# Load casts queued behind their neighbours, second-layer weights over slots 59 to 73, both ends in written order: one change to a two-layer cross-attention kernel

## The chip, the cores and the metric

The kernel runs on one core of one Trainium2 chip. The metric is the device time of one execution in microseconds (us). Five engines work side by side, each through its own instruction queue in order: PE (TensorE, matmuls; its weight loads are listed apart as PEld), DVE (VectorE), ACT (ScalarE), POOL (GpSimd) and SP (SyncE, which here only issues DMAs). ACT issues a few DMAs too. An instruction waits on semaphores for what it reads, and everything behind it on its engine waits with it.

## What is computed

The input is 16 batches of 256 rows and 320 channels, `x`, and a context of 256 rows and 512 channels for each batch. Two cross-attention layers follow each other, 20 heads of 16 channels each. In layer 1 the first 77 context rows are text and the other 179 image tokens; in layer 2 all but the last 4 are text.

```python
# layer 1 (L0)                                   # layer 2 (L1)
text_out = softmax(q_h k_h^T * s) v_h            text_out = softmax(q k_t^T * s) v_t
text_probs = softmax(q k_text^T * s)             qsem = l2norm(probs_t @ text_ehs)     # per head
sem = (text_probs @ text) @ ip^T * s             sem  = qsem @ l2norm(ip_ehs)^T
fused = q_h ip_k_h^T * s + 0.5 * sem             fused = q k_ip^T * s + 0.5 * sem
ip_out = softmax(fused) * mask @ ip_v_h          ip_out = softmax(fused) * mask @ v_ip
out = (text_out + ip_out) @ Wout + bout + x      out = (text_out + ip_out) @ W_out + b_out + x1
```

All is float32. The kernel keeps that precision by splitting operands into a rounded part and a rest (`hi` and `lo`, type fp32r) and multiplying hi by hi, hi by lo and lo by hi.

## The kernel before

**Slots.** A layer has 80 groups: 16 batches of 5 groups of 4 heads. The main loop (the last lines of the function) runs 162 slots, k = 0 to 161. Slot k of layer 1 is `slot0`, of layer 2 `slot1`; NS = 80 is the first slot of layer 2. In a slot, fixed steps stand at fixed places: `score0` or `both1` makes scores of group k+2 (PE L623 or L749) that DVE reduces to row maxima (L624, L625, L750); `maxima0` or `maxima1` turns the maxima with a small matmul (L631), ACT copies them to `mt` (L633), and ACT issues DMAs (L635) that put them into extra rows of `qs`; `turned0` makes the scores again, transposed (L647, tile T), ACT takes the exponential into P (L650), POOL multiplies P by `rs` (L651); `attend0` multiplies by the values (L678), and `settle0` scales the result on DVE. `stacks(k + LEAD)`, LEAD = 4, has SP issue the loads of `qs` and `ks` for a group four slots ahead.

**Tasks.** All else is a generator with a list of due times in slots: `task(key, times, make, *needs)`. `fill(now)` runs, in order of due time, every step that is due; `get` runs a task to its end. `("k0", c)` makes keys of a pair of batches, `q0` queries, `s0` the semantic scores (`rs`), `v0` values, `c0` and `c1` the output projection of a batch (PE L496, residual added in L723), `o1`, `k1`, `t1` the layer-2 inputs, and `i1` layer 2's image softmax (`image_softmax`, L852 to L883), whose result `rs` `close1` multiplies on PE at L892. `w1`, `w6`, `w2`, `w4` load and split weights.

**Loads and casts.** `dma` (L82) puts a load on SP's queue. `in_turn` loads parts of 128x512 into a ring of two raw buffers, then `halves` splits each: an ACT cast (L131), and a DVE or POOL subtraction (L132).

**What sets the order.** PE's queue is in the order written, since the main loop runs under a schedule that pins PE alone. For ACT, DVE, POOL and SP the scheduler chooses the order by times that it reckons while the program is built. The first stretch, `begin()`, pins PE and SP.

**Ends.** `begin()` makes keys, queries, semantic scores and values of the first batches, loads the first four stacks and makes the first maxima, before slot 0. At the other end, slots 160 and 161 finish the last two groups, and `fill(999)` the last image softmax and output projections.

**DVE, POOL and buffers touched.** `bmask` has a buffer of its own, loaded at the start; `settle1` takes a fresh half of `nt` for each group; batch 0's `x` is loaded twice, as `x0` for the queries and in `close0` as the residual.

Of the kernel before, what the change touches and what calls it, by code (L numbers as in the profile page):

```python
# [48 lines left out]
def xattn2(  # L49
# [80 lines left out]
    def halves(hi, lo, src, eng=nc.vector):  # L130
        nc.scalar.copy(hi, src)  # L131
        eng.tensor_sub(lo, src, f(hi))  # L132

    def in_turn(parts, wait, tag="raw", eng=nc.vector):

        ahead = []
        for src, hi, lo in list(parts) + [(None, None, None)]:
            if src is not None:
                raw = buf(tag, [128, 512], bufs=2)
                shape = src.shape  # L140
                raw = raw[:, : shape[1]] if len(shape) == 2 else raw.rearrange("p (k n) -> p k n", k=shape[1])
                dma(raw, src)
                ahead.append((hi, lo, raw))
            if len(ahead) > 1 or (src is None and ahead):
                halves(*ahead.pop(0), eng)
            if wait:
                yield
# [40 lines left out]
    def context(b, n, wait=0):  # L188

        tiles, parts = [], []  # L190
        for k in range(0, 4, 3 - n):
            src = cT_d[:, b * S : (b + n) * S].rearrange("(k p) t -> p k t", p=128)[:, k : k + 3 - n]
            ct = buf("cta" if n == 1 or k < 2 else "ctb", [128, 2, 512], FR, bufs=SIZES["CTA" if n == 1 or k < 2 else "CTB"], name="ct")
            split = lambda t: t.rearrange("p (k t) -> p k t", t=n * S)
            parts.append((src, split(ct[:, 0]), split(ct[:, 1])))
            tiles.append(ct)
        yield from in_turn(parts, wait, "rawc", nc.gpsimd if wait else nc.vector)
        if n == 2:
            return lambda s, k: tiles[k][:, s].rearrange("p (b t) -> p b t", b=2)
        return lambda s, k: tiles[k // 2][:, s, (k % 2) * S : (k % 2 + 1) * S]  # L200
# [65 lines left out]
    bmask = const_tile([128, CP], "bmask")  # L266
# [10 lines left out]
    def keys0(c):  # L277
        if c not in ct0:
            ct0[c] = yield from context(2 * c, 2, 0.25)
        ct = ct0[c]  # L280
        for m in range(3):
            ms = slice(m * 128, (m + 1) * 128)
            kst = buf("kst", [128, 2, 2, S], FR, bufs=SIZES["KST"])
            for w, lo, hi, a, z in ((wk0, 0, 96, 0, T0), (wki0, T0 - 1, S, T0, S)):
                kp = bank()[:, : 2 * (hi - lo)].rearrange("p (b t) -> p b t", b=2)
                prod(kp, lambda s, k: w(s, k, ms), lambda s, k: ct(s, k)[:, :, lo:hi], 4)
                halves(kst[:, 0, :, a:z], kst[:, 1, :, a:z], kp[:, :, a - lo : z - lo])
                if a:
                    keys_out(kd[0][c], m, kst)
                yield  # L290
# [50 lines left out]
    def weights1():  # L341
# [25 lines left out]
        halves(cip[:, 0], cip[:, 1], raw)  # L367
# [38 lines left out]
    def weights3():  # L406
        gm = buf("vr", [128, 3 * (H * V0W + 16)], FR, bufs=3, name="gm")
        gm = gm[:, : 7 * 128].rearrange("p (g n) -> p g n", n=128)
        nc.gpsimd.memset(f(gm), 0.0)
        gmt.append(gm)  # L410
        yield
        if len(gmt) == 2:
            one, two = [buf("rs", [128, 2 * S], bufs=2, name="one") for i in range(2)]
            w1["vb"], w1["mhalf"] = one[:, :CP], one[:, CP : CP + NG * 8]
            w1["pT"], w1["pip"] = two[:, :S], two[:, S:].rearrange("p (f c) -> p f c", c=32)
            dma(bmask, bmask_d)
            nc.vector.memset(w1["mhalf"], -0.5)
            nc.gpsimd.memset(w1["pip"], 0.0)
# [61 lines left out]
    def split(src, neg, eng, tag):  # L480

        hl = buf(tag, [128, 5, S], FR)
        nc.scalar.copy(hl[:, 0:3], src)
        eng.tensor_sub(hl[:, 3:5], src[:, 0:2], f(hl[:, 0:2]))
        nc.vector.scalar_tensor_tensor(  # L485
            hl[:, 2], f(hl[:, 2]), neg, src[:, 2], op0=ALU.mult, op1=ALU.add
        )
        return hl
# [125 lines left out]
    maxes = {}  # L614

    def score0(k, t):
        Q, K = QK[k]
        if t == 0:
            maxes[k] = buf("mn", [128, 2, 4, 2], FR, bufs=2)
        mn = maxes[k]  # L620
        sp = scores()
        for h in range(4):
            mm(sp[:, h], Q[: XROW + T0, h, t * 128 : (t + 1) * 128], K[: XROW + T0, h], start=True, stop=True)  # L623
        nc.vector.tensor_reduce(mn[:, t, :, 0], sp[:, :, :T0], axis=AX.X, op=ALU.max)  # L624
        nc.vector.tensor_reduce(mn[:, t, :, 1], sp[:, :, T0:], axis=AX.X, op=ALU.max)  # L625

    def maxima0(k):
# [6 lines left out]
        for h in range(4):  # L634
            nc.scalar.dma_start(f(Q[XROW + T0 : KS0, h]), f(mt[2 * h : 2 * h + 2]))  # L635

    def turned0(k, t):
# [10 lines left out]
        for p in range(2):  # L648
            pt = P[k, p][:, t]
            nc.scalar.activation(pt, st[p], AF.Exp, scale=SCALE)  # L650
            nc.gpsimd.tensor_mul(pt, pt, rs[:, t : t + 1].to_broadcast([128, 2, S]))  # L651
# [8 lines left out]
    def slot0(k):  # L660
# [4 lines left out]
        yield 0.2  # L665
        if k > 0:
            yield lambda: attend0(k - 1)
        yield lambda: ahead(k + 2, 1)
        yield lambda: turned0(k, 1)
        yield lambda: stacks(k + LEAD)  # L670
# [59 lines left out]
    def both1(k, t):  # L730
# [14 lines left out]
        if a:  # L745
# [4 lines left out]
            nc.vector.tensor_reduce(maxes[k + 2][:, t], sp[:, :, :T1], axis=AX.X, op=ALU.max)  # L750
        if c:
            for u in range(2):
                if t == 0:
                    P[k, u] = buf("P", [128, 2, 2, S], bufs=SIZES["NP"])
                nc.scalar.activation(P[k, u][:, t], st[u], AF.Exp, scale=SCALE)  # L755
# [13 lines left out]
    def rounded1(k, u):  # L769
        R[k, u] = buf("ctb", [128, 2, 2, S], FR, bufs=SIZES["CTB"], name="ph")  # L770
        W[k, u] = buf("wB", [128, 2, 2, S], bufs=SIZES["WB"], name="wt")
        for t in range(2):
            nc.scalar.activation(R[k, u][:, t], P[k, u][:, t], AF.Copy, scale=0.5)  # L773
            nc.gpsimd.tensor_sub(W[k, u][:, t], P[k, u][:, t], f(R[k, u][:, t]))  # L774
# [54 lines left out]
    def settle1(b, g, pv):  # L829
# [4 lines left out]
        na = buf("nt", [128, 2, 8, 32], bufs=2, name="na")[:, 0]  # L834
# [11 lines left out]
    def image_softmax(b):  # L846
        nt, si = norms[b], get("o1", b)[1]
        pool = nc.gpsimd
        small = lambda n, t: buf(t, [128, NG, 8] + ([n] if n > 1 else []))
# [7 lines left out]
        pool.tensor_tensor(r, u, w1["mhalf"].rearrange("p (f s) -> p f s", f=NG), op=ALU.pow)  # L857
        b4 = lambda t: t.unsqueeze(3).to_broadcast([128, NG, 8, NIP])
        a = small(NIP, "a")
        pool.tensor_mul(a, nt[:, :, :, 1:5], b4(r))  # L860
        by_group = lambda t: t[:, :, : NG * NIP].rearrange("p f (g n) -> p g f n", n=NIP)
# [13 lines left out]
        pool.tensor_mul(z4, z4, mk.unsqueeze(1).to_broadcast([128, NG, 8]))  # L875
        pi = w1["pip"]
        pool.tensor_mul(by_group(pi), a, b4(z4))
        vb = w1["vb"]
# [4 lines left out]
        nc.vector.tensor_mul(vb, vb, bmask)  # L883
# [15 lines left out]
    def close0(b):  # L899
        x1 = yield from finish(0, b, results["gathered", 0, b], load(xT_d[b], "xc"))  # L900
        dma(x1d[b].rearrange("(k p) t -> p k t", p=128), x1)

    def open1(b):
# [3 lines left out]
        yield  # L907
        qh, qd = yield from queries(1, xs)
# [57 lines left out]
    first_kt = []  # L966
# [7 lines left out]
    FIRST = {"k0": [-1, -1, -1, -1, -1, 0.6, 1, 1.2, 1.6, 2, 2.4], "s0": [-1, 0.2, 0.2, 0.6, 0.6, 1, 1.2]}  # L974
    for c in range(B // 2):
        n, k = 10 * c, [("k0", c)] if c else []
        task(("k0", c), FIRST["k0"] if c == 1 else shifted(n, -13, -12.6, -12.3, -12, -11.6, -10.8, -10.4, -9.8, -9.4, -8.8, -8.4), (lambda c=c: keys0(c)) if c else first_keys,
             *((("v0", 2 * c - 1), ("m0t", 2 * c - 1), *([("w4", 0)] if c > 1 else [])) if c else ()))
# [6 lines left out]
        for b, t in ((2 * c, (-7.4, -6.4, -6, -5.4, -5, -4.4, -3.4)), (2 * c + 1, (-2.4, -1.4, -1, -0.8, -0.4, 0, 1.2))):  # L985
            task(("s0", b), FIRST["s0"] if b == 1 else shifted(n, *t), lambda b=b: semantic0(b), ("q0", b), ("m0t", b))
            task(("c0", b), shifted(5 * b, *((6, 7, 7.6, 8.2) if b % 2 == 0 else (6, 7.2, 8.2, 9.2) if b < B - 1 else (7, 7.67, 8, 8.67))), lambda b=b: close0(b), ("gathered", 0, b), ("w4", 0))
    for b in range(B):
# [3 lines left out]
        task(("o1", b), shifted(n, -7.67, -7, -6.67, -5.33, -4.33, -4), lambda b=b: open1(b), ("w1",), ("w2",), ("c0", b), *([("o1", b - 1)] if b else []))  # L992
        task(("i1", b), shifted(n, 6.67, 6.67, 6.67, 7.33, 7.33, 7.67, 7.67, 8, 8.33), lambda b=b: image_softmax(b), ("gathered", 1, b), ("taken", B + b - 1))
        task(("c1", b), shifted(n, 8.67, 8.67, 8.67, 8.67, 9, 9.67, 11.67, 13), lambda b=b: close1(b), ("i1", b), ("w4", 1))
    spread = lambda t, d, n: [t + d * i for i in range(n)]
    task(("w1",), spread(62, 0.3, 17), weights1, ("k0", B // 2 - 1))
    task(("w6",), spread(67.2, 0.25, 13), weights6, ("w1",), *[(x, c) for c in range(B) for x in ("v0", "m0t")])
    task(("w2",), spread(70.6, 0.3, 4), weights2, ("q0", B - 1), ("w6",))
# [19 lines left out]
    def begin():  # L1018
# [13 lines left out]
        get("v0", 0)  # L1032
        get("m0t", 1)
        score0(0, 0)
        score0(0, 1)
        parts(k0)
        get("v0", 1)
        maxima0(0)
        stacks0(2)
        score0(1, 0)  # L1040
        score0(1, 1)
        parts(*[("k0", 1)] * 2)
        get(*q1)
        stacks0(3)
        maxima0(1)
# [5 lines left out]
    with tc.manual_schedule(engines=PINNED | {mybir.EngineType.SP}):  # L1051
# [91 lines left out]
```

## Time and profile before

| | |
|---|---|
| median of 3 runs | 1681.77 us (1676.26 to 1691.26) |
| the profiled execution | 1684.64 us; its span, first to last instruction, 1682.9 us |
| PE busy | 1549.7 us, 92%, 13306 matmuls |
| PE weight loads busy | 1246.9 us, 74% |
| DVE busy | 1230.4 us, 73% |
| POOL busy | 1177.6 us, 70% |
| ACT busy | 831.7 us, 49% |
| mean granted PE clock | 0.964 |

The profile lists for each engine when it was busy, and for each idle stretch before an instruction what ended it ("releaser"). A row such as `PE S L623 <- ACT vr L319` says that the PE matmul of line 623, writing S, stood idle until ACT's instruction of line 319 was done. The granted clock (PEclk) is the share of its full clock that PE got; matmuls just after idle time run longer. Busy times are sums, so what matters is where PE, which is busy for 92%, is not.

### The profile page before, as it was taken

The numbers are of one execution on the slowest core, as the hardware profiler recorded it, in microseconds if no ns is written. First come the engines' busy times: TensorE is split into PE (matmuls) and PEld (weight loads), VectorE is DVE, ScalarE is ACT, GpSimd is POOL, SyncE is SP. The second block draws the span as 40 slices with busy tenths as digits, with TensorE's granted clock in tenths as the row PEclk, the third lists the DMA queues.
The fourth block names the chain that finished last, engine by engine and source line by source line (L and its number), as shares of the span: only waits on it lengthen the run. The fifth ranks groups of instructions, "written<-read, shape, count | busy, mean of one in ns | idle before, by whom it ended". The sixth has DMA issues, their size and how long they took to land.

```text
span 1682.9 us, 36242 instructions
## 1 busy us (share of the span) xinstructions
PE 1549.7 (92%) x13306; PEld 1246.9 (74%) x13306; DVE 1230.4 (73%) x2400; ACT 831.7 (49%) x1796; POOL 1177.6 (70%) x1124
## 2 busy tenths in 40 slices
PE   7599999999999898789999999999999999999985
PEld 7587878787778787567777776777777777777754
DVE  5367666767676776768778788788878878787764
ACT  5244444545444544435555544555555555555541
POOL 3367777778776765767587757767876677767774
PEclk9799999999999998899999999999999999999997
DMA  8766767676767675665434323342444334332301
GB/s 253 197 189 193 206 193 207 187 210 194 217 183 207 184 211 150 189 186 152 122 90 136 119 83 107 120 142 77 121 127 128 100 98 137 118 123 61 110 21 33
DMA packets 247742, 247.49 MB, mean 147 GB/s; under 512 B 31050, under 2 KB 231468, under 8 KB 247564
## 3 DMA queue, kind: packets, MB, share of 16 engines
q1 hardware_dynamic: 245324, 243.85, 49.4%
q8 instruction: 106, 1.74, 0.4%
q10 hardware_dynamic: 2240, 1.31, 0.3%
q14 instruction: 72, 0.59, 0.1%
HBM read 121.21 MB, written 88.18 MB: 124 GB/s over the span
## 4 chain that ended last, share of the span: by engine, by line
PE 57%; DMA 14%; DVE 12%; POOL 6%; ACT 4%; issue 3%; SPq 3%; ACTq 1%; POOLq 0%; DVEq 0%
PE X L184 15%; PE X L783 12%; PE X L496 9%; PE P L678 4%; PE S L623 3%; POOL wt L774 3%; PE T L647 3%; SPq L82 3%; PE P L792 3%; PE T L744 3%; DMA qs<-qd 2%; PE P L795 2%; DMA qs<-mt 2%; POOL r L857 2%; DMA ks<-M 2%
## 5 line engine op out<-in xcount | busy, mean ns | idle before, releaser
L651 POOL TENSOR_TENSOR P<-P,rs 128x512 f32<-128x512 f32 x320 | 409.9, 1301 | 162.6 <-ACT P L650 162.2
L774 POOL TENSOR_TENSOR wt<-P,ctb 128x512 f32<-128x512 f32 x320 | 421.6, 1331 | 131.0 <-ACT ctb L773 126.2
L783 PE MATMUL X<-ctb,gm 128*128 128x512 f32 x1120 | 332.5, 415 | 5.0 <-DVE si L915 4.1
L650 ACT ACTIVATE P<-T 128x512 f32<-128x512 f32 x320 | 176.4, 593 | 218.1 <-PE T L647 106.6
L773 ACT ACTIVATE ctb<-P 128x512 fp32r<-128x512 f32 x320 | 196.7, 630 | 77.9 <-PE X L783 59.9
L755 ACT ACTIVATE P<-T 128x512 f32<-128x512 f32 x320 | 174.1, 597 | 121.5 <-PE T L744 98.4
L783 PEld LDWEIGHTS X<-ctb,gm 128*128 128x128 f32 x1120 | 191.2, 190 | 52.6 <-DVE si L915 6.8
L784 DVE TENSOR_TENSOR wt<-X,wt 128x512 f32<-128x512 f32 x320 | 215.9, 676 | 18.1 <-PE X L783 16.4
L750 DVE TENSOR_REDUCE mn<-S 128x4 fp32r<-128x1008 f32 x160 | 191.0, 1194 | 0.4 <-PE S L749 0.3
L623 PE MATMUL S<-ks,qs 125*128 125x256 f32 x640 | 119.9, 312 | 26.9 <-DVE mn L625 8.0
L625 DVE TENSOR_REDUCE mn<-S 128x4 fp32r<-128x716 f32 x160 | 142.7, 892 | 0.0
L647 PE MATMUL T<-qs,ks 127*128 127x256 f32 x640 | 114.4, 294 | 25.6 <-DMA qs<-mt 16.2
L623 PEld LDWEIGHTS S<-ks,qs 125*128 125x128 f32 x640 | 90.5, 199 | 63.5 <-issue 49.2
L678 PE MATMUL P<-P,vr 128*32 128x256 f32 x1920 | 129.3, 402 | 2.8 <-DVE tmp L695 1.7
L496 PE MATMUL X<-ho,wF 128*128 128x256 f32 x768 | 115.9, 293 | 7.6 <-DVE ho L485 3.4
L857 POOL TENSOR_TENSOR r<-u,rs 128x40 f32<-128x40 f32 x16 | 108.4, 6772 | 14.5 <-DVE u L854 14.5
L647 PEld LDWEIGHTS T<-qs,ks 127*128 127x128 f32 x640 | 92.6, 195 | 33.7 <-DMA qs<-mt 13.9
L496 PEld LDWEIGHTS X<-ho,wF 128*128 128x128 f32 x768 | 105.3, 197 | 14.7 <-DVE ho L485 4.6
L496 PE MATMUL X<-hq,wE 128*128 128x256 f32 x768 | 109.2, 286 | 3.5 <-DVE mn L625 2.4
L624 DVE TENSOR_REDUCE mn<-S 128x4 fp32r<-128x308 f32 x160 | 74.9, 468 | 48.0 <-PE S L623 47.5
L184 PE MATMUL X<-cta,wA 128*128 128x252 f32 (+1 forms) x720 | 101.3, 288 | 8.3 <-ACT wA L131 6.0
L496 PEld LDWEIGHTS X<-hq,wE 128*128 128x128 f32 x768 | 102.3, 193 | 6.9 <-issue 2.5
(195 smaller groups left out, 2859.5 us busy)
## 6 DMA issues: line engine op xcount, KB each, us to landing
qd<-q SPq DMA_DIRECT2D x96, 384.0 KB
qs<-tph SPq DMA_DIRECT2D x64, 308.0 KB
kd<-kst SPq DMA_DIRECT2D x73, 256.0 KB
rawc<-in_cT_dram SPq DMA_DIRECT2D x62, 256.0 KB
qs<-qd SPq DMA_DIRECT2D x80, 192.0 KB
ks<-kd SPq DMA_DIRECT2D x80, 192.0 KB
ks<-kd SPq DMA_DIRECT2D x160, 96.0 KB
qs<-qd SPq DMA_DIRECT2D x160, 96.0 KB
```

What stands on the lines that cost most here:

```text
L184: last = mm(out, lhs(a, k), rhs(b, k), start=i == 0, stop=i == len(terms) - 1)
L496: mm(pp, w(s, k, slice(m * 128, (m + 1) * 128)), a[:, t], start=i == 0, stop=i == len(terms) - 1)
L623: mm(sp[:, h], Q[: XROW + T0, h, t * 128 : (t + 1) * 128], K[: XROW + T0, h], start=True, stop=True)
L647: mm(st[p][:, j], K[:KS0, 2 * p + j, t * 128 : (t + 1) * 128], Q[:KS0, 2 * p + j], start=True, stop=True)
L650: nc.scalar.activation(pt, st[p], AF.Exp, scale=SCALE)
L651: nc.gpsimd.tensor_mul(pt, pt, rs[:, t : t + 1].to_broadcast([128, 2, S]))
L678: mm(pv[32 * s : 32 * s + 32, o : o + S], v[:, vt, h : h + 32], P[k, s // 2][:, t, s % 2], start=vt < 2, stop=vt != 1,)
L750: nc.vector.tensor_reduce(maxes[k + 2][:, t], sp[:, :, :T1], axis=AX.X, op=ALU.max)
L773: nc.scalar.activation(R[k, u][:, t], P[k, u][:, t], AF.Copy, scale=0.5)
L774: nc.gpsimd.tensor_sub(W[k, u][:, t], P[k, u][:, t], f(R[k, u][:, t]))
L783: mm(yp, gm[:, gb], R[k, u][:, kt], start=i == 0, stop=i == len(blocks[n]) - 1)
L784: nc.vector.tensor_mul(W[k, u][:, n], yp, W[k, u][:, n])
```

## The change

It has six parts.

1. `queued(inst)` makes an instruction stand, on its engine, behind the last instruction that was marked with `anchor`. Anchors are the reductions to maxima (DVE), the exponentials (ACT), the POOL products with `rs` and, in layer 2, the POOL subtraction of `rounded1`. Queued are the casts and subtractions of loads in `in_turn` (where it waits between parts), those of `split` for queries, and, in `turned0`, the second half's exponential behind the last maxima DMA of the next group.
2. `in_turn` loads two parts ahead and splits a part before it loads the next; the second context (batches 2 and 3) may use two rings, `rawc` and `raw`, and then loads all four parts at once.
3. `weights1` is cut in two. Its first part (`w1`) stands at slots 59.2 to 61.2, the rest (`w7`) from 62.2, `weights6` from 67.2 and `weights2` at 71.6 to 73, three steps in a slot; before they were at 62, 67.2 and 70.6 with 0.25 to 0.3 slots between steps. `keys0` starts 1.4 slots earlier and calls for the earlier values and tokens itself.
4. `begin()` pins all five engines; its parts are in another order, the first two groups' maxima go out by SP's queue instead of ACT's, stacks 2 and 3 are loaded earlier among the SP queue's issues, and batch 0's residual is loaded there. `slot0` moves the stacks of group 5 from slot 1 to slot 2.
5. The last batch's image softmax is cut in two: groups 0 to 3 as task `i1a` at slot 160.1, group 4 afterwards. The output projections `c1` of the last two batches are due 1.67 slots later.
6. `bmask` shares a buffer with `nt` and is loaded at the first `settle1`; `na` uses two halves of one buffer.

```diff
+    def queued(inst, *behind):
+        for other in behind or [anchors.get(inst.ins.engine)]:
+            if other is not None:
+                tc.add_manual_dep(inst.ins, other.ins.name, ..., reason="order")
+        return inst
+
+    def anchor(inst):
+        anchors[inst.ins.engine] = inst
+        return inst
+
+    def halves(hi, lo, src, eng=nc.vector, loaded=False):
+        order = queued if loaded else lambda inst: inst
+        order(nc.scalar.copy(hi, src))
+        order(eng.tensor_sub(lo, src, f(hi)))
...
+            if len(tags) > 1:
+                new = () if i else range(len(parts))
+            else:
+                new = range(i + 1 if i else 0, min(i + 2, len(parts)))
+            if i:
+                halves(*ahead.pop(0), eng, wait)
+            for j in new:
...
-            if len(ahead) > 1 or (src is None and ahead):
-                halves(*ahead.pop(0), eng)
...
-            nc.scalar.activation(pt, st[p], AF.Exp, scale=SCALE)
-            nc.gpsimd.tensor_mul(pt, pt, rs[:, t : t + 1].to_broadcast([128, 2, S]))
+            exp = anchor(nc.scalar.activation(pt, st[p], AF.Exp, scale=SCALE))
+            if t and k + 1 in issues:
+                queued(exp, issues[k + 1])
+            anchor(nc.gpsimd.tensor_mul(pt, pt, rs[:, t : t + 1].to_broadcast([128, 2, S])))
...
-            nc.scalar.dma_start(f(Q[XROW + T0 : KS0, h]), f(mt[2 * h : 2 * h + 2]))
+            issues[k] = queue.dma_start(f(Q[XROW + T0 : KS0, h]), f(mt[2 * h : 2 * h + 2]))
...
-    def image_softmax(b):
-        nt, si = norms[b], get("o1", b)[1]
+    def image_softmax(b, lo=0, hi=NG):
+        gs, n = slice(lo, hi), hi - lo
+        nt, si = norms[b][:, gs], get("o1", b)[1]
...
-        task(("c1", b), shifted(n, 8.67, 8.67, 8.67, 8.67, 9, 9.67, 11.67, 13), ...)
+        task(("c1", b), shifted(n + (1.67 if b > B - 3 else 0), 8.67, 8.67, 8.67, 8.67, 9, 9.67, 11.67, 13), ...)
+    task(("i1a",), [2 * NS + 0.1], lambda: image_softmax(B - 1, 0, NG - 1), ("i1", B - 2))
...
-    task(("w1",), spread(62, 0.3, 17), weights1, ("k0", B // 2 - 1))
-    task(("w6",), spread(67.2, 0.25, 13), weights6, ("w1",), ...)
-    task(("w2",), spread(70.6, 0.3, 4), weights2, ("q0", B - 1), ("w6",))
+    thirds = lambda n, t: [t + i // 3 + (0.2, 0.6, 1.0)[i % 3] for i in range(n)]
+    task(("w1",), thirds(7, 59), weights1)
+    task(("w7",), thirds(13, 62), weights7, ("w1",), ("k0", B // 2 - 1))
+    task(("w6",), thirds(13, 67), weights6, ("w7",), ...)
+    task(("w2",), [71.6, 72, 72.2, 72.6, 73], weights2, ("q0", B - 1), ("w6",))
...
         stacks0(1, "QKT")
         get("v0", 0)
+        v1 = ("v0", 1)
+        stacks0(2)
+        parts(k0)
+        score0(0, 0)
+        parts(v1)
+        score0(0, 1)
         get("m0t", 1)
-        score0(0, 0)
-        score0(0, 1)
-        parts(k0)
-        get("v0", 1)
-        maxima0(0)
-        stacks0(2)
+        maxima0(0, nc.sync)
+        parts(v1)
+        get(*v1)
+        get(*q1)
         score0(1, 0)
+        stacks0(3)
         score0(1, 1)
-        parts(*[("k0", 1)] * 2)
-        get(*q1)
-        stacks0(3)
-        maxima0(1)
+        parts(("s0", 1))
+        maxima0(1, nc.sync)
+        parts(("k0", 1))
+        resid0.append(load(xT_d[0], "xc"))
...
-    with tc.manual_schedule(engines=PINNED | {mybir.EngineType.SP}):
+    with tc.manual_schedule(engines=PINNED | {... for e in ("SP", "Activation", "DVE", "Pool")}):
         begin()
```

## The prediction

> **What bounds the kernel now.** I read the page's slices first, then busy time by stretch, because a mean of 92% for PE says nothing about where the rest is. The page's PE and clock rows:
>
> ```profile
> PE   7599999999999898789999999999999999999985
> ...
> PEclk9799999999999998899999999999999999999997
> ```
>
> PE is not full in three places: the first two slices, slices 14 to 18, and the last. The table of stretches (us; PE, PEld, DVE, ACT, POOL busy; clock; DMA share) gives them sizes:
>
> ```profile
> 0.00:80.00 80.00, 52.95 (x313) 48.70 (x314) 37.74 (x92) 32.98 (x79) 26.03 (x33) 0.88 0.78 227
> 80.00:560.00 480.00, 447.24 (x4029) 382.00 (x4028) 332.81 (x740) 228.45 (x524) 351.71 (x331) 0.97 0.68 197
> 560.00:640.00 80.00, 73.19 (x646) 63.15 (x648) 57.25 (x132) 38.62 (x89) 56.19 (x53) 0.96 0.74 208
> 640.00:780.00 140.00, 113.49 (x985) 92.59 (x979) 99.28 (x202) 60.44 (x133) 98.10 (x92) 0.90 0.58 166
> 780.00:1600.00 820.00, 803.31 (x6881) 618.88 (x6882) 656.44 (x1148) 444.26 (x924) 597.19 (x572) 0.99 0.37 113
> 1600.00:1682.90 82.90, 59.52 (x465) 41.62 (x463) 46.91 (x89) 27.00 (x50) 48.35 (x46) 0.85 0.09 27
> ```
>
> PE's idle time is 27.1 us in the start, 32.8 in layer 1 (6.8%), 6.8 + 26.5 = 33.3 in the crossing to layer 2, 16.7 in layer 2 (2.0%) and 23.4 in the end. So layer 2 is PE's own, and the prizes are the start, the crossing and the end. Whom PE waited for there (total us, times, longest):
>
> ```profile
> PE S L623 <- ACT vr L319: 7.2, 1, 7.2
> ...
> PE T L647 <- DMA qs<-mt: 5.3, 4, 3.3
> ...
> PE S L623 <- DVE mn L625: 8.0, 4, 4.5
> ...
> PE X L892 <- DVE rs L882: 17.6, 2, 11.2
> ```
>
> The first two are of the start, the third of 640 to 780, the fourth of the end. What held ACT in the start and in the crossing, from its waits and its timeline:
>
> ```profile
> ACT wA L131 <- DMA rawc<-in_wk_dram: 6.7, 2, 6.0
> ...
> 53.97 1.26 ACT L131 CAST cta<-rawc 128x512 fp32r<-128x512 f32 x2 [7.39 <-DMA rawc<-in_cT_dram]
> 55.14 0.43 ACT L319 ACTIVATE vr<-X 128x320 f32<-128x320 f32 x1
> 55.46 0.34 ACT L633 CAST mt<-X 8x256 fp32r<-8x256 f32 x1
> 59.03 4.88 ACTq L635 DMA_DIRECT2D qs<-mt  x4
> ```
>
> The cast of a load that had not landed stood ahead of two copies out of PSUM that PE needed, and PE stopped for 7.2 us. The same shape shows at 641: ACT waits 6.0 us for a weight load, DVE's subtraction L132 waits 5.5 for that cast, the reductions L624 and L625 stand behind it, and PE waits 4.5 for them.
>
> **The start.** In the changed program's order the casts of the second context stand on ACT behind the first four exponentials, so the 7.2 us go. The eight maxima DMAs go to SP. The first four stand after SP instruction 59, a place that SP reached at about 46 before, now with a few issues other than before ahead of it: out at about 48 to 51 instead of 59.0 to 63.9. From issue to matmul took 3.9 us (59.03 to 62.91), so the first T matmul stands at 52 to 54 instead of 62.9. What is late next is SP, which issued almost without a pause from 36.1 to 59: behind the four come three q writes (1.9 us), four stack loads (4.1), two kb loads (0.9), four more maxima (at 0.57 to 1.22 each by ACT's row: 2.3 to 4.9) and only then the second context's four loads, at 61 to 65 instead of 48 to 63. With casts of 0.62 and POOL subtractions of 1.25 each, the last is split at about 70 to 71; PE took those keys at 70.95 before. So of the 20 us that PE idled after 38 us, I leave 13 or 14: -6 us. Bounds: -12 (the context lands in time) to +3 (it lands 3 us later than the old place).
>
> Against this part speaks the Trainium skill, "DMA: Bandwidth & Descriptors", section "Issuing engines are not separate DMA queues": SP's and ACT's DMAs run on the same 16 engines, and issuing from two saves only the issue time. By it the move to SP gives back what two queues saved, 4.6 to 9.8 us of issue time by the rows above, and the start would end near 0 instead of -6.
>
> **Layer 1, 80 to 560.** PE's order differs only in one projection moved by 0.2 slots for each even batch. Query casts now stand behind an exponential, and the last maxima DMA ahead of the second exponential, so ACT waits (if a DMA issue waits) with the exponential behind it. The waits that these touch are T on qs<-mt, 9.0 us in 13, and T on ACT's P, 7.7 in 6. I take -2, with -8 (half of both) and +6 (as much again for the issue wait).
>
> **The crossing, 560 to 780.** Nineteen weight and token loads with their casts (ACT 0.2 to 0.62, DVE 0.41 to 1.76 each) are the same work, from slot 59 to 73 instead of 62 to 71.5, each behind a reduction or an exponential. Two stalls are plainly of the removed kind: 4.6 us at 577.6 (a product over a loaded tile, L348, ahead of the reductions on DVE) and 4.5 at 641.3. After each the matmuls ran slowly: from 645.8 nine groups took 9.7 us that take 5.6 at full clock, from 582.2 another 1.7 too much. That is 9.1 + 5.8 = 15. The other 24.2 us of idle time are short waits on DVE and ACT; at layer 1's rate of 6.8%, 15 stay, and 9 could go, with some 7 of slow clock behind them. Spreading thins the load only by 14 slots against 10, so I take a quarter of those 16: 4. Sum -19. Bounds: -35 (all down to layer 2's rate, 33.3 - 4.5, and some clock) to +5 (new waits; see the rivals).
>
> **Layer 2.** PE's and POOL's orders are the same up to the last batches. `bmask` moves one DMA of 0.59 us on SP, and `nt` keeps its depth of two. Zero, plus or minus 4.
>
> **The end.** PE waited 6.4 us at 1636.95 for the softmax of batch 14, and 11.2 at 1668.77 for that of batch 15. The first product now stands 1.67 slots later (about 8 us each), behind 14 POOL products instead of 9: POOL's work from the start of `pow` is 14 x 1.27 + 6.8 + 3.2 = 28 us, so 1614.7 + 28 = 1642.5, against PE's arrival near 1644. The wait goes, with 1.5 us of cover; each us that POOL is later comes back. For the last batch, `pow` (L857) costs 6.77 us for 40 elements. Cut into 32 and 8, by element 5.4 and 1.35; the large part starts at about 1645.5, once DVE's L854 has passed the additions for batch 14. It ends near 1651, seven small POOL steps of 0.2 to 0.5 follow, the small `pow` ends near 1654.5, and four more steps, exponential and transposition (1664.2 to 1668.8 took 4.6) bring L892 to about 1658.5, 10 us sooner than 1668.77; the 14 us behind it stay. If `pow` has a fixed price, 6.77 twice, 6.8 of the 10 are lost. So -10, from -13 to -3.
>
> **Sum.** -6 - 2 - 19 + 0 - 10 = -37. Against the profiled execution's 1684.64 (span 1682.9 and 1.7 around it) that is 1647.6; the median, 1681.77, lies 2.9 lower, so 1645.
>
> **The rivals.**
>
> *Waiting in written order (slower).* A raw ring holds two buffers. SP issues the next part only when DVE has subtracted the last but one, and DVE now does that behind a reduction, which waits for PE. The stack loads of `qs` and `ks` stand behind on SP. If they come late, PE waits as it did on qs<-qd, up to 1.8 us at a time (80 to 560). Nineteen loads at 1.8 are 34 us in place of the crossing's -19; with -18 elsewhere the kernel is at 1681.8 + 16 = 1698. It decides from about ten such waits on, where the rest is eaten up. Against it: stacks are issued four slots (35 us) ahead, and PE waited on qs<-qd only 0.7 us in 640 to 780.
>
> *DVE is the bound in the crossing.* DVE is busy 71% there, POOL 70%, and nearly all of PE's waits in 640 to 780 are on DVE or ACT work that is not removed. Then a stall taken away is found again a slot later: crossing 0 to -6, sum -18 to -24: 1658 to 1664. For it: in 640 to 780 nine more waits on mn beside the long one, 10.1 us in all.
>
> *The whole first half runs freely.* Idle time of start, layer 1 and crossing goes down together: -12 - 8 - 35 - 13 = -68, 1614. For it: many small stalls start with one long one; against: layer 1's waits are on DMA, which stays 68% busy.
>
> *The start gives nothing,* for SP is its bound: the rule above. Then 1651, inside the forecast.
>
> **How the numbers follow.** Forecast, 1632 to 1658: 0.60, likeliest 1645. DVE-bound crossing, 1658 to 1672 with a start or end at its poor bound: 0.20. Free first half: 0.08. Written-order waits, above 1672: 0.12. The range takes the forecast and most of the second case, with part of the third: 1622 to 1668. A measurement of this kernel tells about 1% from no change, so faster by over 1% means below 1665: 0.60 + 0.08 + half of the second, 0.78. Slower by over 1%, above 1698.6, is the bad half of the rival, 0.08; the same takes 0.14.
>
> **What would show it.** In the profile after: no cast with a wait on rawc of over 3 us ahead of a copy out of PSUM; no L319 wait of 7 us; first T matmul before 56; SP without a pause to 65; PE idle below 20 us in the crossing; L892 without a wait but the last, which is under 8 us, and two `pow` of 5.4 and 1.35. I am wrong if PE waits for qs<-qd or ks<-kd in the crossing, if the small `pow` takes 6.8, or if layer 1's idle share rises above 6.8%.

## The result, and the profile after

The changed kernel took 1643.07 us (median, 1638.19 to 1646.88) where the kernel before took 1686.51 on the same chip: a ratio of 0.974, 95% interval 0.970 to 0.978. Its profiled execution took 1646.73 us with a span of 1644.9, against 1684.64 and 1682.9 before. The forecast was 1645, from a profiled 1647.6.

So the sum held, but its terms did not. I cut both traces at the same matmuls: the starts of the value products of groups 7, 57 and 79 (`attend0`) and, in layer 2, of groups 0 and 71 (`attend1`).

| stage (us) | before | changed | difference | predicted |
|---|---|---|---|---|
| start, to group 7 | 144.3 | 144.1 | -0.2 | -6 |
| layer 1, groups 7 to 57 | 429.1 | 413.5 | -15.6 | -2 |
| crossing, groups 57 to 79 | 212.4 | 208.9 | -3.5 | -19 |
| layer 2, group 79 to its group 71 | 798.2 | 791.9 | -6.3 | 0 |
| end, from its group 71 | 99.0 | 86.5 | -12.5 | -10 |

The page's PE and clock rows of the changed kernel:

```profile
PE   7789999999999899689999999999999999999996
...
PEclk9799999999999999789999999999999999999998
```

Slice 2 is 7 now and was 5, slice 40 is 6 and 8 in the clock, was 5 and 7. But slice 17, in the crossing, reads 6 with a clock of 7, and was 7 with 8: the hole there is still open. Three rows of the table of stretches (us; PE, PEld, DVE, ACT, POOL busy; clock; DMA share):

```profile
80.00:560.00 480.00, 451.58 (x4135) 388.03 (x4134) 337.62 (x761) 233.99 (x541) 365.48 (x342) 0.98 0.72 204
560.00:640.00 80.00, 70.90 (x625) 60.92 (x624) 57.28 (x132) 39.15 (x91) 53.55 (x49) 0.94 0.70 203
640.00:780.00 140.00, 117.43 (x1029) 94.16 (x1029) 103.80 (x204) 63.23 (x139) 101.55 (x99) 0.89 0.61 177
```

From 560 to 780 PE is idle for 9.1 + 22.6 = 31.7 us, against 33.3 before, though the crossing itself now begins 16 us earlier. From 80 to 560 it is idle for 28.4, against 32.8, and its clock is 0.98, not 0.97. PE's waits (total us, times, longest), in order the start, layer 1, 560 to 780 and the end:

```profile
PE X L571 <- DMA kb<-kd: 10.8, 2, 5.6
...
PE T L673 <- DMA qs<-mt: 8.9, 11, 1.3
...
PE T L673 <- DVE tmp L726: 9.8, 2, 5.9
...
PE X L931 <- DVE rs L921: 6.7, 1, 6.7
```

Gone are the 7.2 us on the values' copy (L319 before, L343 now), layer 1's 7.7 us on exponentials and one of the two waits for an image softmax. The first row grew: the semantic matmuls (L571, L545 before) wait for their keys, 5.6 us at 59.7 and 5.2 at 102. The second wait stood in the kernel before too, where the row was:

```profile
PE X L545 <- DMA kb<-kd: 3.9, 1, 3.9
```

New is the one at 59.7; SP issued that load at 59.65, behind the first maxima and the stack loads. And the crossing has a single wait of 5.9 us, longer than the 4.6 of before behind the same instruction, DVE's square of a loaded tile (L372, L348 before).

The casts still wait for their loads, too. ACT waited 4.9 us for a part of `wki` and 4.0 for a part of `wv`. The second of these, and what stood behind it:

```profile
655.79 0.46 ACT L147 CAST wC<-rawc 128x320 fp32r<-128x320 f32 x1 [3.95 <-DMA rawc<-in_wv_dram]
...
656.28 0.49 DVE L148 TENSOR_TENSOR wC<-rawc,wC 128x320 fp32r<-128x320 f32 x1 [2.56 <-ACT wC L147]
...
658.62 0.28 PE L657 MATMUL X<-ident_r,mn 128*8 128x128 f32 x1 [2.90 <-DVE mn L651]
```

### The profile page after: what moved, and what is told of

It is laid out like the page before. It is cut to its first block, busy times and chain, and to the rows that moved or that the text cites. A ratio compares the mean times of both kernels' runs of the same rounds, so it can differ in the third digit from the quotient of the medians.

```text
span 1644.9 us, 36268 instructions
## 1 busy us (share of the span) xinstructions
PE 1539.0 (94%) x13306; PEld 1239.6 (75%) x13306; DVE 1197.1 (73%) x2404; ACT 830.3 (50%) x1797; POOL 1184.0 (72%) x1131
## 4 chain that ended last, share of the span: by engine, by line
PE 54%; DVE 14%; DMA 10%; POOL 9%; ACT 5%; issue 4%; SPq 2%; ACTq 0%; POOLq 0%; DVEq 0%
PE X L205 16%; PE X L814 10%; PE X L522 7%; PE P L709 5%; POOL wt L805 4%; PE S L649 3%; PE P L823 3%; PE T L673 3%; DMA qs<-qd 3%; PE P L826 3%; PE T L775 2%; DMA qs<-mt 2%; DVE ho L512 2%; DMA kd<-kst 2%; DVE wt L815 2%
## 5 line engine op out<-in xcount | busy, mean ns | idle before, releaser
L814 PE MATMUL X<-ctb,gm 128*128 128x512 f32 x1120 | 328.8, 412 | 2.5 <-DVE wt L815 2.5
L649 PE MATMUL S<-ks,qs 125*128 125x256 f32 x640 | 119.1, 310 | 11.2 <-DVE mn L651 3.5
L894 POOL TENSOR_TENSOR r<-u,rs 128x40 f32<-128x40 f32 (+2 forms) x17 | 108.7, 6393 | 14.8 <-DVE u L891 14.7
```

What stands on the lines that cost most here:

```text
L814: mm(yp, gm[:, gb], R[k, u][:, kt], start=i == 0, stop=i == len(blocks[n]) - 1)
```

## The experiments

The kernels were measured in three groups of four, each beside the kernel before on one chip, where that took 1693.2, 1682.8 and 1690.3 us; so times are given as ratios to it (e1 to e4 are the first group; the changed kernel again, e5, e6 and e7 the second; e8 to e11 the third; the row "changed" is the result above). Stages are from one profile each: start (to group 7), layer 1, crossing, layer 2 (here its groups 0 to 71), end.

| kernel | ratio (95%) | start | layer 1 | crossing | layer 2 | end |
|---|---|---|---|---|---|---|
| before | 1 | 144.3 | 429.1 | 212.4 | 788.1 | 99.0 |
| changed | 0.974 (0.970 to 0.978) | 144.1 | 413.5 | 208.9 | 781.8 | 86.5 |
| changed, again | 0.978 (0.973 to 0.984) | 145.3 | 416.8 | 205.7 | 782.0 | 85.5 |
| e1: no queuing | 0.982 (0.978 to 0.986) | 145.4 | 420.4 | 201.1 | 798.7 | 86.9 |
| e2: before, and queuing | 1.007 (1.004 to 1.010) | 148.3 | 444.1 | 218.7 | 782.0 | 97.4 |
| e3: old weight slots | 0.973 (0.970 to 0.976) | 145.9 | 416.7 | 204.3 | 781.8 | 85.5 |
| e4: old start | 0.978 (0.974 to 0.981) | 151.1 | 413.8 | 210.9 | 781.7 | 86.5 |
| e5: old end | 0.986 (0.980 to 0.991) | 145.4 | 417.1 | 208.9 | 781.7 | 97.5 |
| e6: before, and two loads ahead | 0.998 (0.995 to 1.002) | 145.9 | 427.1 | 213.6 | 799.1 | 98.6 |
| e7: e1, doubling by ACT | 0.976 (0.970 to 0.983) | 146.8 | 423.6 | 204.5 | 774.0 | 86.3 |
| e8: query splits not queued | 0.980 (0.976 to 0.984) | 143.4 | 430.6 | 201.0 | 783.6 | 86.0 |
| e9: queuing to slot 79, doubling by ACT | 0.970 (0.966 to 0.973) | 143.4 | 415.0 | 211.8 | 773.9 | 84.3 |
| e10: e9, weights not queued | 0.973 (0.970 to 0.977) | 149.0 | 416.2 | 204.4 | 774.1 | 85.6 |
| e11: weights' rests by ACT | 0.971 (0.967 to 0.975) | 143.1 | 415.5 | 203.7 | 780.9 | 86.5 |

**The changed kernel again**, for the scatter of the stages.

> The changed kernel once more, to see how far its stages differ from one profile to another. From the three kernels run so far that share its first 58 slots or more: layer 1 (groups 7 to 57) 413 to 421, crossing 201 to 211, both together 618 to 626, layer 2 (batch groups 0 to 71) 781.5 to 782.5, end 86 to 87.

All as expected but the end, 85.5 for 86 to 87. Counting e4, e5 and e9 too, which share its order in layer 1 and the crossing (e3 in layer 1), equal stretches of program differ by up to 3.6 us in layer 1 and 6.1 in the crossing, but by 0.3 in layer 2 where it is queued. A stage's difference below that says little by itself; where the same wait comes and goes with it, it says more.

**The queuing, taken away and put in alone** (e1, e2).

```diff
         for other in behind or [anchors.get(inst.ins.engine)]:
-            if other is not None:
+            if False:
```

> The changed kernel without its first part: casts, query splits and exponentials stand where the scheduler puts them; PE's order is the same. Layer 1 is measured from the value products of group 7 to those of group 57 (before 429.1 us, changed kernel 413.5), the crossing from group 57 to 79 (212.4 and 208.9). Theory A: layer 1's 15.6 us came from the queuing; then layer 1 takes 424 to 432 here, the crossing 212 to 225, and the kernel 1655 to 1675. Theory B: they came from the other parts (two loads ahead, the DMAs' places); then layer 1 stays at 411 to 417 and the kernel at 1640 to 1650. Theory C: the two profiles differ by chance; then any value between, and the time within 5 us of the changed kernel's 1643.

> The kernel before with the first part alone, queuing. Theory A: layer 1 (groups 7 to 57) falls from 429.1 to 411 to 419, the crossing by 0 to 8, start, layer 2 and end stay: 1660 to 1675. Theory B: layer 1 stays at 425 to 432 and the kernel within 6 us of 1683. A third way: without two loads ahead the queued casts hold up the next load, and the kernel is slower than before, 1690 or more.

Theory A fell by e2, where the third way came: the queuing alone makes the kernel slower (1704.1 us beside 1693.2), by 15 us in layer 1. What PE waits for there:

```profile
PE X L200 <- POOL ctb L148: 17.4, 10, 2.6
```

A queued POOL subtraction (L148) of the context comes too late for the keys and values (L200): the load was issued only when its buffer came free, and the subtraction stands behind a product as well. In the changed kernel's layer 1 no such row exists; there `in_turn` loads two parts ahead and contexts start 1.4 slots earlier (which of the two removes it was not tried). By e1 the queuing is worth 3 to 10 us in layer 1 (420.4, in e7 423.6, against 413.5 to 417.1) on top of the other parts. It fits neither A nor B as written: the crossing became shorter without it, not longer, and layer 2 lost 17 us, which I had not foreseen (below).

**Two loads ahead alone** (e6: the new `in_turn`, the context's two rings and its earlier slots, put into the kernel before).

> The kernel before with the second part alone: two loads ahead, contexts 1.4 slots earlier, the second context on two rings. Without the queuing and without the weight spread the stretch from group 7 to 79 was 621 to 625 us in every kernel that had this part (641.5 before, 662.8 with queuing alone). Theory D, that this part alone brought what layer 1 and the crossing gained: 618 to 628 here and the kernel 12 to 22 us below before. Theory A (the queuing): 636 to 646, and the kernel within 5 us of before. Waits of 3.2 us on nothing shown in layer 2 stay by either, 2 to 5 of them.

Theory D fell too: no stage became shorter beyond scatter. So loading two ahead brings nothing by itself, and the queuing by itself costs 21 us from group 7 to group 79; together they gain. e6 also gives the kernel before a second set of stages, within 2 us but for layer 2.

**The query split out of the queuing** (e8).

```diff
-        order = queued if tag == "hq" else lambda inst: inst
+        order = lambda inst: inst
```

> The changed kernel with the three instructions of the query split (ACT's cast of 0.84 us, POOL's subtraction, DVE's) out of the queuing; loads stay queued. Layer 1 (groups 7 to 57) takes 413.5 to 417.1 us with the whole queuing, 420.4 and 423.6 without it. If the query split is what the queuing wins in layer 1: 420 to 425, and DVE's part of it takes about 1.0 us again instead of 0.49. If the casts of the contexts are: 413 to 418.

Layer 1 took 430.6, above both ranges: the queuing's gain there hangs on the three instructions of the query split, and with the loads alone queued layer 1 is longer than with nothing queued (420.4, 423.6). PE's longest row in layer 1, and then one of its waits in the timeline (start, us, engine, line, output from input, idle before):

```profile
PE T L673 <- ACT P L676: 16.6, 11, 3.3
```

```profile
316.98 4.70 ACTq L661 DMA_DIRECT2D qs<-mt  x3
...
321.78 1.08 ACT L676 ACTIVATE P<-T 128x512 f32<-128x512 f32 x2 [6.91 <-DMA qs<-mt]
...
322.43 0.99 PE L673 MATMUL T<-qs,ks 127*128 127x256 f32 x4 [3.28 <-ACT P L676]
```

ACT's exponentials stand behind its own DMA issues; three of those took 4.7 us (one is 0.57 as a rule), the exponentials came 6.9 us late, and PE's T banks stayed full. That is the row of 7.7 us on ACT's P that the kernel before had. The DMAs of the maxima share ACT's queue with the exponentials, so the row must be read together with T's wait for these DMAs. Both rows in the kernel before, and in e1, where nothing is queued:

```profile
PE T L647 <- DMA qs<-mt: 9.0, 13, 1.3
PE T L647 <- ACT P L650: 7.7, 6, 1.5
```

```profile
PE T L673 <- DMA qs<-mt: 16.0, 17, 1.6
...
PE T L673 <- ACT P L676: 0.6, 2, 0.4
```

Together T's waits on the two are 16.3 to 16.7 us from group 7 to group 57 in the four kernels that queue nothing (before, e1, e6, e7), 20.8 in e8, and 5.7 to 9.2 in the nine profiles with the whole queuing there. The sum is what the queuing halves; without it the wait only passes from one row to the other. In e8 DVE's part of the split took 0.82 us (median) instead of the changed kernel's 0.49; in the kernel before 1.04. Why just these issues of ACT took so long is not shown.

**The weights at their old slots** (e3; `w6` and `w2` go back to 67.2 and 70.6 in the same way).

```diff
-    task(("w1",), thirds(7, 59), weights1)
-    task(("w7",), thirds(13, 62), weights7, ...)
+    task(("w1",), spread(62, 0.3, 7), weights1)
+    task(("w7",), spread(63.8, 0.3, 13), weights7, ...)
...
```

> The changed kernel with the weights of layer 2 due where they were before (from slot 62 on, 0.25 to 0.3 slots apart). Forecast of the prediction (each stall removed is worth its length): the crossing takes 215 to 225 instead of 208.9 and the kernel 1650 to 1660. The rival (DVE and ACT are the bound in the crossing, so that spreading only moves the stalls): the crossing takes 205 to 213 and the kernel 1640 to 1648.

As the rival's forecast had it for the kernel (1644.8 us): the spreading is worth nothing once the casts are queued, the crossing took 204.3, and the time is the same (0.973 for 0.974 and 0.978). Without queuing it seems to matter. From group 7 to group 79, layer 1 and crossing together, neither takes 641.5 (before) and 640.7 (e6), spreading alone 621.5 and 628.1 (e1, e7), queuing alone 621.0 (e3), both 622.4 to 626.8 (the changed kernel twice, e4, e5, e9). So the two look like substitutes; but e1 and e7 also have two loads ahead and the new start, so their row is not the spreading alone.

**The start of before** (e4: the old `begin()`, its slots, group 5's stacks in slot 1).

> The changed kernel with the start of before: old order of begin(), the first maxima issued by ACT, PE and SP alone pinned, group 5's stacks in slot 1, batch 0's residual loaded later. Forecast of the prediction: group 7's value products start 4 to 9 us later than the 144.1 of the changed kernel, and the kernel takes 1647 to 1652. The rival, that the start gives nothing: 143 to 146 again, and 1641 to 1646.

Group 7 came at 151.1: against the changed kernel's 144.1 the old start costs 7.0 us, in the predicted range. The other profiles with the new start and the query split queued have 143.1 to 145.9 (149.0 in e10), so 5 to 8. The whole kernel's ratio, 0.978, doesn't show it: the changed kernel had 0.974 and 0.978. And the kernel before, with that same start, had 144.3. PE's waits in e4, to 151:

```profile
PE S L649 <- ACT vr L343: 6.1, 1, 6.1
PE X L571 <- DMA kb<-kd: 5.9, 1, 5.9
PE T L673 <- DMA qs<-mt: 5.1, 3, 4.1
```

The first and third are the two waits that the prediction had shown, 7.2 and 5.3 us, and the new start does remove them (no row on L343 left, 0.8 on qs<-mt). The other parts, though, had made the start 6.8 us longer (144.3 to 151.1; queuing alone 148.3 in e2, two loads ahead alone 145.9 in e6). And the new order pays with one more wait for `kb`, the 5.6 us at 59.7; that of 5.9 in e4 stands at 106, where the kernel before has its own.

**The end of before** (e5).

> The changed kernel with the end of before: the last image softmax in one piece, the last two output projections at their old slots. Forecast of the prediction: PE waits again for the softmaxes of batches 14 and 15, together 14 to 19 us, and the kernel takes 8 to 14 us longer than the changed one. Rival: the last batch's chain was shortened by something else (the queue order of POOL), and the wait for batch 15 stays under 8 us, the kernel within 4 us.

12.5 us longer than the changed kernel in the same group (1661.3 against 1648.8), as forecast. PE's waits in e5's end, and POOL's `pow` (L894) in the changed kernel's (partitions x elements, busy us, mean ns):

```profile
PE X L931 <- DVE rs L921: 17.7, 2, 11.2
```

```profile
L894 POOL TENSOR_TENSOR r<-u,rs 128x40 f32<-128x40 f32 x1 | 6.8, 6774 | 0.2 <-DVE u L891 0.2
L894 POOL TENSOR_TENSOR r<-u,rs 128x32 f32<-128x32 f32 x1 | 5.4, 5440 | 0.8 <-DVE u L891 0.8
L894 POOL TENSOR_TENSOR r<-u,rs 128x8 f32<-128x8 f32 x1 | 1.6, 1647 | 0.1
```

The price goes by element, 0.16 to 0.17 us each, with 0.3 to 0.4 us fixed. Batch 14's wait is gone whole, batch 15's fell from 11.2 to 6.7.

**Where layer 2's time went** (e7). In e1 PE stood still five times for 3.2 us in layer 2, in e6 four times, in the kernel before twice; in no kernel that queues there (e2 to e5, e8, e11, the changed one). The trace names no releaser ("issue"). One of them in e1's timeline:

```profile
899.56 3.93 DVE L489 TENSOR_SCALAR gm<-gm 128x128 fp32r<-128x128 f32 x1
...
900.48 2.50 POOL L805 TENSOR_TENSOR wt<-P,ctb 128x512 f32<-128x512 f32 x2
...
902.92 0.49 POOL L914 TENSOR_TENSOR rs<-a,z 128x160 f32<-128x160 f32 x1
903.41 0.47 DVE L754 SCALAR_TENSOR_TENSOR xc<-X,bo,xc 128x256 f32<-128x256 f32 x1
...
903.99 0.50 PE L780 MATMUL S<-ks,qs 48*128 48x256 f32 x4 [3.24 <-issue]
```

DVE's doubling of a 128x128 tile runs from 899.56 until POOL's unbroken run of instructions ends at 903.41; everything behind it on DVE is late, and PE with it. All five stalls look like that. But a run of POOL doesn't always hold the doubling to its end; the next one in e1:

```profile
955.73 2.55 POOL L148 TENSOR_TENSOR cta<-rawc,cta 128x512 fp32r<-128x512 f32 x2
...
957.52 0.84 DVE L489 TENSOR_SCALAR gm<-gm 128x128 fp32r<-128x128 f32 x1
...
958.21 0.29 POOL L912 TENSOR_TENSOR z<-z,mk 128x40 f32<-128x40 f32 x1
```

Here POOL ran on without a gap, and the doubling was done 0.08 us after the end of the POOL instruction that it had met. e7 moves the 16 doublings to ACT and leaves PE's, POOL's and SP's orders as they were in e1:

```diff
-                nc.vector.tensor_scalar_mul(G[:, 5, :], f(G[:, 5, :]), 2.0)
+                nc.scalar.activation(G[:, 5, :], f(G[:, 5, :]), AF.Copy, scale=2.0)
```

> The kernel without queuing (e1) with one thing moved: the doubling of a 128x128 tile in tokens1 (16 instructions in all) is done by ACT instead of DVE. PE's, POOL's and SP's orders stay as they were. In e1 PE stood idle 3.2 us five times in layer 2, each time while DVE's doubling took 3.9 us instead of 0.39 beside POOL's additions and products. Theory of the blocked port (DVE's instruction is held as long as POOL works through two products on its other side): the five waits vanish, layer 2 takes 781 to 784 instead of 798.7, and the kernel 1642 to 1652. Rival (the doubling is only where it shows; another DVE instruction is held instead, or PE waits on something else): three or more waits of about 3 us stay, layer 2 takes over 790.

All five waits vanished, and the kernel took 1646.5 us, with no queuing as fast as the changed kernel in the same group (1648.8). Layer 2 took 774.0, below the forecast and 8 us less than queued. No run has both the queuing in layer 2 and the doubling on ACT, so which of the two these 8 us hang on is not shown. The doubling's row (min/median/max ns) in e1 and in the changed kernel; on ACT it took 302 to 312 ns:

```profile
L489 DVE TENSOR_SCALAR gm<-gm x16: 386/841/3943, 749.1 to 1577.8; 128x128 fp32r<-128x128 f32 x16
```

```profile
L489 DVE TENSOR_SCALAR gm<-gm x16: 311/321/540, 749.6 to 1558.6; 128x128 fp32r<-128x128 f32 x16
```

**A version of both** (e9, e10): queuing only below slot 80, the doubling on ACT; e10 frees the weights' casts too.

```diff
-            if other is not None:
+            if other is not None and clock[0] < NS:
```

> The changed kernel with the queuing only in layer 1 and the crossing, none from slot 80 on, and the doubling in tokens1 done by ACT. Theory of the blocked port: layer 2 takes 773 to 776 as in e7 (782.0 with the queuing), layer 1 and crossing stay at 413 to 417 and 205 to 209, so the kernel is 6 to 9 us below the changed one, 1634 to 1643. Rival: it was the earlier weights or another order that made e7's layer 2 short; 780 to 783 here and no gain.

> e9 with the weights' casts and subtractions out of the queuing as well; contexts and query splits stay queued. So far the crossing took 213 us with neither queuing nor spreading (before 212.4, e6 213.6), 201 and 204.5 with spreading alone, 204.3 with queuing alone, 205.7 to 210.9 with both. If the two stand in for each other and queuing what is spread already costs a little: 200 to 204 here, and 3 to 6 us below e9. If those differences are chance: 205 to 209 and within 2 us of e9.

e9 took 1638.47 us where the kernel before took 1690.26, a ratio of 0.970 (0.966 to 0.973), the lowest of all; layer 2 took 773.9 as expected, the crossing 211.8, above the range. The intervals of the changed kernel's 0.974 and 0.978 overlap with it, so that it beats it rests on layer 2's 8 us, seen in e7, e9 and e10 alike. e10 fits neither forecast: its crossing is 7 us shorter than e9's, but its start is 5.6 us longer (the first output weights, due at slots 2.6 to 3.2, are freed as well; whether they do it was not tried), and in all it was slower: 1643.5.

**Is DVE the bound in the crossing?** (e11)

```diff
-        order(eng.tensor_sub(lo, src, f(hi)))
+        if loaded and eng is nc.vector and clock[0] > 50:
+            order(nc.scalar.copy(lo, src))
+        else:
+            order(eng.tensor_sub(lo, src, f(hi)))
```

> The changed kernel with the weights' subtractions of the crossing and the second layer (DVE, 0.41 to 1.76 us each) replaced by a second ACT cast; so the rest part of those weights is the rounded part once more, and layer 2's numbers change. DVE loses some 20 instructions. If DVE is the bound in the crossing (71% busy, waits on its maxima): 190 to 200 us instead of 205 to 209, the kernel 1630 to 1640. If the bound is no single engine's load: 203 to 210, the kernel 1640 to 1650.

DVE was busy 138.3 us in the crossing instead of 151.3, yet the crossing took 203.7, 2 us below the shortest with the changed kernel's order. 13 us off DVE's load came through as 2 to 8, so DVE's load as a whole is not the bound. What goes together with the crossing's length are two single stalls: the row "T on DVE tmp L726" of the changed kernel, 9.8 us in two waits, stands with the same numbers in all profiles that share its order (205.7 to 211.8). Where one of the two is left, in e3, e10 and e11 (5.8 to 6.1 us), the crossing took 203.7 to 204.4; where the row is 0.9 or none, in e1, e7 and e8, 201.0 to 204.5. No run took away one of the stalls alone, so this is argued from the rows, not shown. The longer one, in the changed kernel's timeline and, for the square (L372), by its line:

```profile
560.74 0.58 SPq L82 DMA_DIRECT2D rawc<-in_cip_dram  x1
...
565.03 1.06 DVE L372 TENSOR_TENSOR rawc<-rawc 64x512 f32<-64x512 f32 x1 [3.39 <-issue]
...
568.01 0.35 DVE L726 TENSOR_TENSOR tmp<-nt,P 128x256 f32<-128x256 f32 x1
...
568.42 1.22 PE L673 MATMUL T<-qs,ks 127*128 127x256 f32 x4 [5.89 <-DVE tmp L726]
```

```profile
L372 DVEq EVENT_SEMAPHORE  x1: 4924/4924/4924, 560.1 to 560.1; - x1
```

The square of a loaded tile stands ahead of `settle0`'s products (L724, L726) and the reductions. From 560.1 it waits 4.9 us on a semaphore, while SP issues its load only at 560.74, and DVE is idle for 3.4 of them. `weights1` issues it directly; it isn't among the queued. In e1 and e7 it waits 3.4 and 3.1 us and still costs PE one stall of 3.3, listed under `mn`; in e8 it stands where PE has no wait over 2.5 us behind it. Loading the tile (`cipn`, L369) a slot earlier may be a remedy; it was not tried.

## Why the prediction was right, and which terms were wrong

**The sum** came out at -38.0 for -37, because the misses cancelled: +15.5 in the crossing and +5.8 in the start against -13.6 in layer 1, -6.3 in layer 2 and -2.5 in the end. That was luck in the terms, not in the direction: no stage lost. (The stages here end at groups, those of the prediction at round times.)

**The start, -6.** Right as the worth of the new order (7.0 by e4, 5 to 8 by the other profiles), wrong as a stage (-0.2), because I priced the new order against the trace of before and not against one in which queuing and earlier context loads stretch the start by 6.8. I had listed the `kb` loads among what SP issues, but put no price on PE's wait for them: 5.6 us at 59.7, and 5.2 instead of 3.9 at 102. SP was later than I reckoned as well: the first four maxima DMAs went out at 51.2 to 53.8, for an estimated 48 to 51. The rival "the start gives nothing" named the result, by another cause.

On the rule that the prediction set against this part, the Trainium skill, "DMA: Bandwidth & Descriptors", section "Issuing engines are not separate DMA queues": no run here moved the maxima DMAs alone, so it is neither borne out nor refuted.

**Layer 1, -2.** The term that was mis-sized most on the good side: -12 to -16. The two waits that I named, T on qs<-mt and on ACT's P, fell from 16.7 to 8.9 us (8.0 in the second profile): that is my bound of half of both, -8, where I took -2. The mechanism is right, since the sum is about halved in every kernel with the whole queuing and in none without (e1, e6, e7, e8). PE's idle time there went from 28.8 to 21.5 us. What I had no term for is PE's busy time, which fell as much again in the first profile (400.3 to 392.0) and half as much in the second (396.0). It doesn't take the queuing: e1 has 392.4 without it. Its cause is not shown. I also priced the pieces as if each stood alone, while e2, e6 and e8 show that single pieces cost up to 15 or bring nothing, and the set gains.

**The crossing, -19.** The step that failed is "two stalls are plainly of the removed kind". The first, 4.6 us on the square of L348, was never queued: the diff marks only casts and subtractions, and in the changed order the same instruction costs 5.9. The second, at the weights, shrank from 4.5 to 2.9 us, with ACT still waiting 4.9 and 4.0 us for weight loads, and 3.9 us follow at 664.3 behind a subtraction of the same weights: a cast that is queued behind its neighbours can still come up before its load has landed. The slow matmuls behind the two stalls, 5.8 of the 15 us, stayed too: PE's mean clock in the crossing is 0.90 (0.92 in the second profile), and was 0.92. And the 4 us for the spreading were worth nothing (e3). The rival "DVE is the bound" had the size (0 to -6; -0.6 to -6.7 over the five profiles of this order), but e11 speaks against its cause: with 13 us less on DVE the crossing came 2 to 8 shorter, at 203.7, not at 190 to 200. Single stalls on DVE fit the rows better than its load; no run tested them one by one.

**Layer 2, 0.** I looked at PE's and POOL's order alone. The stalls on "issue", twice 3.2 us, stood in the trace of before, and I had not asked who was running then. By e7 they are DVE's doublings, which POOL holds; in the changed order none of the 16 takes over 0.54 us.

**The end, -10.** Right, and the mechanism with it: -12.5, and e5, with the old end, 12.5 longer. The small `pow` cost 1.65 for an estimated 1.35.

**The written-order rival.** PE did not wait on qs<-qd in the crossing, and the kernel got faster. Its mechanism is real all the same: e2, where loads wait for queued subtractions, takes 21 us more from group 7 to group 79, and PE's waits for the context there add up to that. In the changed kernel, with loads two ahead, they are gone.

Of the signs, these failed: two casts waited over 3 us on rawc; PE idled 31.7 us in the crossing, not below 20; and, by a hair, the first T matmul stood at 56.06 (said: before 56). These held: no wait of 7 us on L343, no pause of SP over 0.5 us from 37 to 69, no qs<-qd or ks<-kd waits in the crossing, one wait at L931 of 6.7, two `pow` of 5.4 and 1.65, layer 1's idle share at 5.9%.

## What to carry to other kernels

Price a removed stall only after checking that the very instruction which holds the queue is among those the change moves. Parts of a schedule aren't additive: from group 7 to 79 queuing alone cost 21 us and loading ahead alone gained nothing, and together they gained; measure each alone and all but each. And where PE waits on nothing that the trace names, look for an instruction of another engine that runs ten times its usual time. With no queuing at all, moving that one instruction to another engine gave the changed kernel's time (e7).

## What the runs showed of the hardware

This DVE instruction between SBUF tiles is held by POOL's work: the doubling took 0.32 us at the median in the changed kernel, 0.84 at the median and 3.9 at most in e1. In the eleven profiles that have the doublings on DVE, 175 of 176 end 0.08 to 0.09 us after the end of a POOL instruction, the short ones too; the one that doesn't (e11) took 0.22 us. DVE's part of the query split, with two SBUF inputs, took 1.04 us before and 0.49 in the changed kernel, where the queuing put it elsewhere. The Trainium skill, "SBUF — State Buffer", section "Who interferes with whom", says that DVE's second port pair is GpSimd's, and that the one that comes second is blocked for the other's whole instruction. The traces agree: of the 48 doublings in before, e1 and e6, 37 end just after the first POOL instruction to end beside them, though POOL goes on. With one thing more: the other 11, as at 899.56, were held through the rest of one and four more, until POOL's first gap. What decides between the two is not shown.

And queued layer 2 repeats itself: its 71 groups took 781.7 to 782.0 us in six profiles of five kernels (780.9 and 783.6 in e11 and e8, which change a part of it), while unqueued, with the doubling on DVE, they took 788.1, 798.7 and 799.1.
